# A two-layer decoder on one core: the last unit of the first mixture in two halves of its positions, and the batch attention of the first blocks among the experts of the second half

## The chip, the cores and the metric

One core of a Trainium2 chip runs the whole network as one program, in fp32. The metric is the device time of one execution in microseconds (us). The profile is one execution recorded by the hardware profiler; its times count from the start of its span.

Engines in the text: PE multiplies matrices, DVE and POOL work on vectors, ACT evaluates functions and copies, SP issues most DMAs. Matmul results land in PSUM, which has eight banks of 128 x 512 fp32.

## The reference

The input x has 16 batches of 128 positions of width 128. Every sublayer is added to its input and normalised. The first layer has an attention by a triangular recursion, a cross attention to a context, and a mixture of experts; the second has an attention, a linear mix with the context, and another mixture. Cut to what matters here:

```python
# first layer, mixture: two of 8 experts for each row, and one shared expert
logits = xf @ gate_w.T
topk_logits, topk_idx = jax.lax.top_k(logits, 2)
topk_w = jax.nn.softmax(topk_logits)
comb = zeros(N, 8).at[arange(N)[:, None], topk_idx].add(topk_w)
for e in range(8):
    g = xf @ wg[e].T                 # 128 -> 192
    u = xf @ wu[e].T
    out = out + comb[:, e:e + 1] * (silu(g) * u @ w_down[e].T)
shared = silu(xf @ sg_gate.T) * (xf @ sg_up.T) @ sg_down.T
x = layernorm(x + shared + out)

# second layer, attention: the first axis of x, the batches, is the sequence;
# 16 heads of width 8, separately at each of the 128 positions
qkv = einsum('sbe,fe->sbf', x, in_proj_weight)
probs = softmax(einsum('sbhd,tbhd->bhst', q, k) / sqrt(8))
x = layernorm(x + einsum('bhst,tbhd->sbhd', probs, v) @ out_weight.T)

# second layer, the rest
x = layernorm(x + part1(x) + mean_of_context_part + b)
x = layernorm(x + top1_of_8_experts(x))          # gelu, 128 -> 512 -> 128
```

## The kernel before

The 16 batches are handled in four units of four batches (512 rows; a unit is `g4` in the code, `G = 4`, `NS = 3` is the number of the last). The first two sublayers run unit by unit. A tile scheduler sees all steps in the order in which the functions issue them and reorders within what its own costs and the dependencies allow; each engine then executes its list in order. `weave(one, other)` issues two lists of steps in proportion, one step of the first and then its share of the second.

**The first mixture** works in two ways.

- Units 0 to 2 are routed. Their rows, sorted by expert, fill 31 tiles of 128 rows (`NT0`), handled in eight quads, the last of three tiles. For tile `j`, `fetch(j)` has SP load the weights of its expert in three DMAs (`wu`, and `wd` twice) into one of eight buffers. `gather` lets POOL collect the rows; `up(q)` flips them, multiplies up and calls `gated` (SiLU on ACT, product on DVE); `scatter(q)` multiplies down, copies the result out of PSUM (`y`, L1199) and lets POOL scatter it to memory (`ys`, L1202). `tiles(q)` issues the up of quad q, then the down and scatter of quad q-1, and then the fetches that need the buffers which this down frees.
- Unit 3 is dense. All eight experts run over all its rows, and each result is added to `acc` with its weight from `comb`. `dense(e)` issues the up of expert `e` at full width (three matmuls of 128x512, in PSUM banks `pg_e`, `pu_e`, `pt_e`), then the down of expert `e-1` (eight matmuls of 128x128 into `py_e`, L1109 and L1110), then four additions on DVE. All PSUM tiles of this stage turn through eight shared banks.

`combine(g4)` reads the two results of each row of a routed unit back (`both`, by ACT's queue or SP's, L1211), adds them with eight DVE instructions (L1218), and normalises into `x3`. `by_position(g4)` flips `x3` on PE (L197) and copies it (L198) to `x3p`, laid out as feature, position, batch.

The sequence at the end of the mixture is:

```python
choices()
up_all(f"s{NS}", sup, NS); tiles(3); down_all(NS)
weave([tiles 4 .. 8], [dense 0 .. 3])
weave([dense 4 .. 8], [combine 0, combine 1, by_position 0, combine 2, by_position 1, by_position 2])
layernorm(x3[NS], acc[NS], ..., act=True)
by_position(NS)
```

**The batch attention** needs all 16 batches of a position, so nothing of it starts before the last `by_position`. It has four blocks of 32 positions (`PB`), and seven stages for each, each named by a letter:

- I, `inputs`: q, k, v of the block (L1286 to L1289), and masked copies of q (`qm`) and v (`vm`).
- S, `both_scores`: 256 small score matmuls, `psc` (32x64 with 16 columns, L1317), and the softmax on DVE, ACT and POOL.
- T, `turn_`: the weights flipped on PE (`pbt`, L1345) and copied out.
- M, `mixed`: 256 small matmuls of weights and v (`pbo`, L1361), combined to `ob`.
- P, `project`: the output projection plus the residual (`pob`), and a layernorm.
- L, `linear` (`pc`, L1401), and G, `logits` (`plr`, L1413): the linear sublayer, and the routing logits `lg` of the last mixture.

A PSUM pool `bpsum` opens for it, with 4 banks for `in` (I and M), 2 for `sc` (scores) and 2 for `rest` (T, P, L, G). The order of the stages is written out as words:

```
I0 I1 S0 I2 S1 T0 M0 I3 S2 T1 P0 M1 S3 T2 P1 M2 L0 T3 P2 M3 L1 G0 P3 L2 G1 L3 G2 G3
```

After G3 come the sort by expert and the last mixture.

Of the kernel before, what the change touches and what calls it, by code (L numbers as in the profile page):

```python
# [9 lines left out]
F32 = mybir.dt.float32  # L10
# [12 lines left out]
G = 4  # L23
NG = B // G
E = 8
# [23 lines left out]
def tile_decoder(ctx: ExitStack, tc: tile.TileContext, a, out):  # L49
# [778 lines left out]
    def routed(g4):  # L828

        flip(x2T[g4], x2[g4], f"x2_{g4}", where=where[0])  # L830
        ps = bank([128, G, E], f"plg_{g4}", *where[0])
        for g in range(G):
            PE.matmul(ps[:, g, :], lhsT=x2T[g4][:, g, :], rhs=gw, start=True, stop=True)
        V.tensor_copy(lg0[:, g4 * G : (g4 + 1) * G, :], ps)
# [228 lines left out]
    def by_position(g4):  # L1063
        flip(
            x3p[:, :, g4 * G : (g4 + 1) * G].rearrange("p t g -> p g t"), x3[g4], f"x3_{g4}",
            S.copy if g4 % 2 else V.tensor_copy,
        )


    with tc.tile_pool(name="mix", bufs=2, side="right") as mp:  # L1070
# [14 lines left out]
        h2s = [mp.tile([128, 512], F32, bufs=1, name=f"h2_{k}") for k in range(4)]  # L1085
# [7 lines left out]
        def gated(key, pg, pu, pt, n, kind):  # L1093
            h1 = mp.tile([128, 512], F32, tag=f"h1_{kind}", name=f"h1_{key}")
# [18 lines left out]
        def up_all(key, ws, g4):  # L1113
# [6 lines left out]
            gated(key, pg, pu, pt, 512, 1)  # L1120

        def shared(g4):
            up_all(f"s{g4}", sup, g4)
            if g4:
                down_all(g4 - 1)

# [10 lines left out]
        def dense(e):  # L1137

            if e < E:
                up_all(f"e{e}", dup[:, e], NS)  # L1140
            if not e:
                return
            py = down(f"e{e - 1}", [ddn[:, e - 1]] * G, G)
            for g in range(G):
                V.scalar_tensor_tensor(
                    acc[NS][:, g], py[:, g], comb[:, g, e - 1 : e], acc[NS][:, g], ALU.mult, ALU.add
                )

# [90 lines left out]
        for q in range(4):  # L1239
# [6 lines left out]
        up_all(f"s{NS}", sup, NS)  # L1246
        tiles(3)
        down_all(NS)
        FIRST = 4
        weave(  # L1250
            [(tiles, q) for q in range(4, nq + 1)], [(dense, e) for e in range(FIRST)],
        )
        weave(
            [(dense, e) for e in range(FIRST, E + 1)],
            [(combine, 0), (combine, 1), (by_position, 0), (combine, 2), (by_position, 1),
             (by_position, 2)],
        )
        layernorm(x3[NS], acc[NS], f"x3_{NS}", act=True)
        by_position(NS)
    last.close()  # L1260

    banks.close()
    banks = ExitStack()
    psum[:] = [banks.enter_context(tc.tile_pool(name="bpsum", bufs=2, space=bass.MemoryType.PSUM))]
    last = ExitStack()  # L1270
    lp = last.enter_context(tc.tile_pool(name="last", bufs=2, side="right"))
    with tc.tile_pool(name="batt", bufs=2, side="right") as bp:
# [5 lines left out]
        PB = 32  # L1278
        qms, kps, vms, pss, wgt, turned, ots_, x4s = {}, {}, {}, {}, {}, {}, {}, {}

        def inputs(k):


            xs_ = x3p[:, k * PB : (k + 1) * PB, :].rearrange("p t s -> p (t s)")
            pq, pk, pv = (bank([128, 512], f"p{n}_b{k}", "in", 4) for n in "qkv")
            PE.matmul(pq, lhsT=ipw[:, 0:D], rhs=xs_, start=True, stop=True)  # L1286
            PE.matmul(pk, lhsT=ipw[:, D : 2 * D], rhs=xs_, start=True, stop=True)  # L1287
            for b in range(4):
                PE.matmul(  # L1289
                    pv[:, b * D : (b + 1) * D], lhsT=xs_[:, b * 128 : (b + 1) * 128],  # L1290
                    rhs=ipw[:, 2 * D :], start=True, stop=True,
                )
            qm = qms[k] = bp.tile([128, PB, 4, B], F32, tag="qm", name=f"qm_{k}")
            for q in range(4):
                src = pq.rearrange("p (t s) -> p t s", s=B)
                if q % 2:
                    S.mul(qm[:, :, q, :], src, quarter[:, q : q + 1])
                else:
                    V.tensor_scalar(qm[:, :, q, :], src, quarter[:, q : q + 1], None, ALU.mult)
            kp = kps[k] = bp.tile([128, PB, B], F32, tag="kp", name=f"kp_{k}")  # L1300
            S.copy(kp.rearrange("p t s -> p (t s)"), pk)
# [323 lines left out]
```

## Time and profile before

| | us |
|---|---|
| median of three runs | 976.67 |
| lowest and highest | 974.72, 983.05 |
| time of the profiled run | 976.67 |
| span of the profiled run | 975.0 |
| granted clock of PE over the span | 0.886 of full |
| busy of the span: PE, DVE, POOL, ACT | 809.9, 648.3, 499.8, 477.8 |
| last copy of a routed tile's result out of PSUM starts | 730.82 |
| first combine of a routed unit starts | 741.87 |
| block 0 of the batch attention starts | 768.18 |

The span goes from the first to the last recorded event; the run's own time is 1.67 us longer. "PEclk" or "granted clock" is the share of full speed that the throttle let PE have, and its single values are 1.00 and 0.50. A line of the timeline gives the start, the length, the engine, the line in the code, the operation, its result and operands by name, and in brackets the idle time before it with what ended it. A line of the waits gives what an engine waited for: the sum, how often, and the longest.

### The profile page before, as it was taken

What the parts mean: (1) busy time and instruction counts of PE and PEld (TensorE: products, weight loads), DVE (VectorE), ACT (ScalarE), POOL (GpSimd) and SP (SyncE); (2) the same over time, 40 slices, a digit from 0 to 9 for tenths busy, and PEclk for the clock granted to TensorE, in tenths of its full rate; (3) what the DMA queues carried; (4) which work ended last, traced back from release to release, by engine and by line L of the source; (5) the groups of instructions that cost most, each with busy time, mean ns of one, the idle gap of its engine ahead of it and who ended that gap; (6) DMA issues with size and microseconds to landing.
All of it is one profiled execution on the core that took longest, in us unless ns stands there. A gap on an engine that the chain in (4) does not pass through costs nothing. (4 is left out here: it accounts for less than half of the span.)

```text
span 975.0 us, 33400 instructions
## 1 busy us (share of the span) xinstructions
PE 809.9 (83%) x13626; PEld 602.7 (62%) x13626; DVE 648.3 (66%) x1875; ACT 477.8 (49%) x1617; POOL 499.8 (51%) x669
## 2 busy tenths in 40 slices
PE   4898789999999998999988788588899798771993
PEld 2545257667576676766666567467776487660893
DVE  4258878897797977988665768755357555636452
ACT  5351055354663547544465775545225523540683
POOL 5288766695586946878642413375441010002653
PEclk9689799899998999999997988988999757775897
DMA  4000000000000000000100000175532000006680
GB/s 111 21 0 1 0 2 4 3 3 2 3 4 3 3 2 3 4 3 3 47 23 24 13 14 13 34 221 112 160 101 66 1 4 4 3 1 188 197 251 15
DMA packets 35273, 40.64 MB, mean 42 GB/s; under 512 B 6495, under 2 KB 25454, under 8 KB 35120
## 3 DMA queue, kind: packets, MB, share of 16 engines
q1 hardware_dynamic: 27808, 29.75, 10.0%
q0 software_dynamic: 3456, 6.22, 2.9%
q10 hardware_dynamic: 3856, 2.52, 0.9%
q8 instruction: 108, 1.77, 0.8%
q14 instruction: 45, 0.37, 0.1%
HBM read 33.98 MB, written 5.41 MB: 40 GB/s over the span
## 5 line engine op out<-in xcount | busy, mean ns | idle before, releaser
L561 ACT ACTIVATE ls<-psl,mx 128x8 f32<-128x8 f32 (+15 forms) x512 | 156.8, 317 | 118.1 <-DVE mx L558 104.7
L568 POOL TENSOR_TENSOR ls<-ls,sm 128x32 f32<-128x32 f32 (+15 forms) x128 | 86.2, 673 | 144.8 <-DVE sm L565 125.9
L582 ACT COPY pt<-psp 32x512 f32<-32x512 f32 (+3 forms) x128 | 73.9, 577 | 72.6 <-PE psp L576 72.2
L561 ACT ACTIVATION_READ_ACCUMULATOR ls<-psl,mx 128x1 f32 x512 | 103.9, 203 | 0.0
L509 PEld LDWEIGHTS psl<-kT,qp 32*32 32x32 f32 x3840 | 66.8, 108 | 52.2 <-issue 20.3
L576 PE MATMUL psp<-ident,ls 128*64 128x128 f32 (+3 forms) x512 | 86.0, 292 | 11.8 <-POOL ls L568 9.4
L509 PE MATMUL psl<-kT,qp 32*32 32x8 f32 (+14 forms) x3840 | 88.8, 223 | 4.9 <-DVE psl L538 2.6
L509 PE MATMUL psu<-kT,qp 32*32 32x8 f32 (+13 forms) x3584 | 81.6, 220 | 9.7 <-DVE kT L550 9.1
L463 POOL TENSOR_TENSOR zi<-X,w 128x512 f32<-128x512 f32 x56 | 71.0, 1267 | 29.1 <-PE psq L465 22.8
L509 PEld LDWEIGHTS psu<-kT,qp 32*32 32x32 f32 x3584 | 65.0, 109 | 23.2 <-DVE kT L550 13.0
L465 PE MATMUL psi<-zi,same 128*128 128x512 f32 x128 | 71.7, 643 | 6.6 <-POOL zi L463 3.8
L576 PEld LDWEIGHTS psp<-ident,ls 128*64 128x64 f32 (+3 forms) x512 | 49.1, 122 | 29.8 <-POOL ls L568 12.9
L435 POOL TENSOR_TENSOR pr<-X,raw 128x64 f32<-128x64 f32 (+7 forms) x64 | 55.6, 871 | 19.5 <-DVE X L479 18.8
L463 POOL TENSOR_TENSOR zq<-X,w 128x64 f32<-128x64 f32 (+7 forms) x64 | 55.2, 863 | 7.3 <-PE psk L465 3.6
L525 DVE TENSOR_TENSOR qp<-X,quarter 128x512 f32<-128x512 f32 x48 | 58.7, 1239 | 0.0
L558 DVE TENSOR_REDUCE mx<-psl 128x4 f32<-128x32 f32 (+15 forms) x128 | 55.0, 430 | 3.9 <-PE psl L509 3.4
L1488 POOL DMA_INDIRECT xin<-xs,takes x23 | 21.9, 953 | 67.3 <-DMA w<-in_f_w 58.3
L465 PE MATMUL psq<-zq,same 128*128 128x64 f32 (+7 forms) x128 | 47.3, 453 | 9.5 <-DVE X L479 5.8
L550 DVE COPY kT<-psu 128x32 f32<-128x32 f32 (+13 forms) x112 | 44.5, 398 | 13.9 <-PE psl L509 9.4
L463 POOL TENSOR_TENSOR zk<-K,w 128x64 f32<-128x64 f32 (+6 forms) x56 | 49.0, 874 | 9.0 <-PE psi L465 7.9
L471 DVE TENSOR_TENSOR psi<-psi,wb 128x512 f32<-128x512 f32 x64 | 44.3, 692 | 12.8 <-PE psi L465 12.6
L590 PE MATMUL pso<-pt,vals 64*32 64x128 f32 (+3 forms) x1024 | 40.6, 304 | 9.9 <-ACT pt L582 9.9
(455 smaller groups left out, 1989.3 us busy)
## 6 DMA issues: line engine op xcount, KB each, us to landing
w<-in_f_w SPq DMA_DIRECT2D x46, 256.0 KB, 4.3
wu<-in_m_up SPq DMA_DIRECT2D x31, 192.0 KB, 2.6
wd<-in_m_dn SPq DMA_DIRECT2D x31, 64.0 KB, 2.0
dup<-in_m_up SPq DMA_DIRECT2D x4, 384.0 KB, 6.6
xs<-x5w SPq DMA_DIRECT2D x4, 264.0 KB
ctxT<-in_ctxT SPq DMA_DIRECT2D x4, 256.0 KB, 5.0
mi<-in_mask SPq DMA_DIRECT2D x4, 256.0 KB, 3.0
both<-ys ACTq DMA_DIRECT2D x2, 512.0 KB, 5.2
```

The source lines that it names most:

```text
L435: P.tensor_tensor(pairs[r][:, j:C, j % 4, :], X[r][:, j:C, :], bc(raw[:, j, :], 1, C - j), ALU.mult)
L463: P.tensor_tensor(z[:, :n], src, bc(w[:, r, s, :], 1, n), ALU.mult)
L465: PE.matmul(flat2(ps[:, :n]), lhsT=same, rhs=flat2(z[:, :n]), start=True, stop=True)
L471: V.tensor_tensor(ps[:, :n], ps[:, :n], bc(wb[:, r, s, :], 1, n), ALU.mult)
L509: PE.matmul(ps[js, g, : keys[g].shape[-1]], lhsT=ws_[js, g].rearrange("p q k -> p (q k)"), rhs=keys[g][js], start=True, stop=True,)
L525: (P if g4 == NG - 1 else V).tensor_tensor(qp[:, k], bc(src.rearrange("p s n -> p n s"), 2, 4), bc(bc(quarter, 1, 4 * G), 3, C), ALU.mult,)
L550: V.tensor_copy(kr[:, :, :i, :].rearrange("p g c k -> p g (c k)"), pu[:, :, :n])
L558: V.tensor_reduce(mx, pl[:, :, :m], AX.X, ALU.max, negate=True)
L561: S.activation(ls[:, g, :m], pl[:, g, :m], AF.Exp, bias=mx[:, g : g + 1], accum_out=sm[:, g : g + 1],)
L568: P.tensor_tensor(ls[:, :, :m], ls[:, :, :m], bc(sm, 2, m), ALU.mult)
L576: PE.transpose(pp[:, g, :], ls[:, g, :n], ident)
L582: S.copy(pt[:n, :, :, ks], pp.rearrange("p g (h k) -> p g h k", k=C))
```

## The change

The last unit of the mixture is worked in two halves, `h = 0` for positions 0 to 63 and `h = 1` for positions 64 to 127 of its four batches. Its transposed rows `x2T[3]` are laid out half by half. `dense(h, e)` runs the shared expert first and then the eight experts over the 256 rows of one half. The gate and up results of a step share one bank (`pgu`); a second bank, `rest_`, holds the third up matmul's result and the down's result of the step before. The residual enters through a matmul with the identity, and DVE copies the shared result to `acc`.

Half 0 stands where the shared expert and the first dense experts stood: its first four steps among quads 3 to 7 and the last scatter, its other steps among the combines. Then a PSUM pool `mpsum` replaces the eight shared banks: one bank each for the two dense tags, 3 for `in`, 2 for `sc`, 1 for `rest`. Half 0 is normalised and flipped. Now the second half's dense steps are woven with stages of blocks 0 and 1 of the attention, whose positions lie in half 0: I0 S0 I1 T0 S1 M0 P0 T1. After the second half's norm and flip the old pool `bpsum` opens, and the remaining stages follow in a new order.

The functions of the attention stages are moved ahead of the mixture unchanged, apart from the numbers of banks, which come from `beside`, and apart from `x4T`, `x5T` and `yc`, which live in a pool of their own (`tail`). The core of the diff:

```diff
     def routed(g4):
...
+            flip(
+                flat(x2T[g4]).rearrange("p (h g t) -> p g h t", h=2, g=G), x2[g4], f"x2_{g4}",
+                lambda dst, ps: S.copy(dst, ps.rearrange("p g (h t) -> p g h t", h=2)),
+                where=where[0],
+            )
...
+    def half_by_position(h, place):
+
+        ps = bank([128, 2, 128], f"fl_x3_{NS}_{h}", *place)
+        for k in range(2):
+            PE.transpose(ps[:, k, :], x3[NS][:, 2 * h + k, :], ident)
+        V.tensor_copy(
+            x3p[:, h * 64 : (h + 1) * 64, BS:].rearrange("p t g -> p g t"),
+            ps.rearrange("p k (g t) -> p (k g) t", g=2),
+        )
...
+        def up_half(key, ws, h, rest):
+
+            pgu = bank([128, 2, 256], f"pgu_{key}", *dense_banks[0])
+            pt = rest[:, 0]
+            for ps, c in ((pgu[:, 0], 0), (pt, 2), (pgu[:, 1], 1)):
+                PE.matmul(
+                    ps, lhsT=ws[:, c * 128 : (c + 1) * 128],
+                    rhs=flat(x2T[NS])[:, h * 256 : (h + 1) * 256], start=True, stop=True,
+                )
+            gated(key, pgu[:, 0], pgu[:, 1], pt, 256, 1)
...
-        def dense(e):
-
-            if e < E:
-                up_all(f"e{e}", dup[:, e], NS)
+        def dense(h, e):
+
+
+            order = [E] + list(range(E))
+            rest = bank([128, 2, 256], f"rest_{h}_{e}", *dense_banks[1])
+            if e <= E:
+                n = order[e]
+                up_half(f"e{h}_{n}", sup if n == E else dup[:, n], h, rest)
             if not e:
                 return
-            py = down(f"e{e - 1}", [ddn[:, e - 1]] * G, G)
-            for g in range(G):
+            n = order[e - 1]
+            h1, h2 = hid.pop(f"e{h}_{n}")
+            py = rest[:, 1].rearrange("p (k d) -> p k d", k=2)
+            ws = sdn if n == E else ddn[:, n]
+            for k in range(2):
+                ts, i = slice(k * 128, (k + 1) * 128), 2 * h + k
+                if n == E:
+
+                    PE.matmul(py[:, k], lhsT=x2T[NS][:, i], rhs=ident, start=True, stop=False)
+                PE.matmul(py[:, k], lhsT=h1[:, ts], rhs=ws[:, 0], start=n < E, stop=False)
+                PE.matmul(py[:, k], lhsT=h2[:, ts], rhs=ws[:, 1], start=False, stop=True)
+            if n == E:
+                V.tensor_copy(acc[NS][:, 2 * h : 2 * h + 2], py)
+                return
+            for k in range(2):
+                i = 2 * h + k
                 V.scalar_tensor_tensor(
-                    acc[NS][:, g], py[:, g], comb[:, g, e - 1 : e], acc[NS][:, g], ALU.mult, ALU.add
-                )
+                    acc[NS][:, i], py[:, k], comb[:, i, n : n + 1], acc[NS][:, i], ALU.mult, ALU.add
+                )
+
+        def half_norm(h):
+            hs = slice(2 * h, 2 * h + 2)
+            layernorm(x3[NS][:, hs], acc[NS][:, hs], f"x3_{NS}_{h}", 2, act=True)
...
         choices()
-        up_all(f"s{NS}", sup, NS)
-        tiles(3)
-        down_all(NS)
         FIRST = 4
         weave(
-            [(tiles, q) for q in range(4, nq + 1)], [(dense, e) for e in range(FIRST)],
+            [(tiles, q) for q in range(3, nq + 1)], [(dense, 0, e) for e in range(FIRST)],
         )
         weave(
-            [(dense, e) for e in range(FIRST, E + 1)],
-            [(combine, 0), (combine, 1), (by_position, 0), (combine, 2), (by_position, 1),
-             (by_position, 2)],
+            [(dense, 0, e) for e in range(FIRST, E + 2)],
+            [(combine, 0), (combine, 1), (by_position, 0), (combine, 2), (by_position, 1)],
         )
-        layernorm(x3[NS], acc[NS], f"x3_{NS}", act=True)
-        by_position(NS)
+
+        banks.close()
+        banks = ExitStack()
+        psum[:] = [banks.enter_context(tc.tile_pool(name="mpsum", bufs=1, space=bass.MemoryType.PSUM))]
+        dense_banks[:] = ("du", 1), ("dt", 1)
+        beside.update({"in": 3, "sc": 2, "rest": 1})
+        half_norm(0)
+        weave(
+            [(dense, 1, 0), (by_position, 2, ("rest", 1)), (dense, 1, 1),
+             (half_by_position, 0, ("rest", 1))]
+            + [(dense, 1, e) for e in range(2, E + 2)] + [(half_norm, 1)],
+            [(mark, 0)] * 4 + [(stages[w[0]], int(w[1])) for w in "I0 S0 I1 T0 S1 M0 P0 T1".split()],
+        )
+        half_by_position(1, ("rest", 1))
     last.close()
...
+    beside.update({"in": 4, "sc": 2, "rest": 2})
...
-            "I0 I1 S0 I2 S1 T0 M0 I3 S2 T1 P0 M1 S3 T2 P1 M2 L0 T3 P2 M3 L1 G0 P3 L2 G1 L3 G2 G3"
...
+        for word in "M1 L0 P1 I2 I3 S2 L1 T2 G0 S3 M2 G1 T3 P2 M3 L2 P3 G2 L3 G3".split():
```

`mark` does nothing: the four marks keep the first four steps of the second list empty.

## The prediction

> **What bounds the kernel now.** I read the page first (PE busy 83% of the span, the critical chain spread over many lines, no engine full), then cut the stretch that the change touches into stages, and asked the busy table for each. Columns: stretch, length, busy us of PE, of its weight loads, of DVE, ACT, POOL, granted clock, DMA share, GB/s.
>
> ```profile
> core 0: us, PE busy (x) PEld busy (x) DVE busy (x) ACT busy (x) POOL busy (x), PEclk, DMA share, GB/s
> 681.00:731.00 50.00, 44.28 (x302) 35.93 (x301) 20.69 (x36) 13.29 (x23) 23.62 (x24) 1.00 0.45 131
> 731.00:742.00 11.00, 11.00 (x51) 6.88 (x50) 4.40 (x10) 3.56 (x6) 2.95 (x3) 1.00 0.32 99
> 742.00:768.00 26.00, 18.58 (x93) 11.89 (x91) 22.59 (x96) 18.25 (x31) 0.25 (x4) 0.89 0.06 20
> 768.00:815.00 47.00, 44.27 (x1137) 35.27 (x1138) 24.37 (x47) 17.56 (x30) 4.14 (x4) 0.70 0.01 3
> 815.00:851.00 36.00, 27.28 (x1074) 24.90 (x1055) 21.12 (x86) 17.36 (x40) 4.15 (x4) 0.76 0.02 4
> 851.00:879.00 28.00, 19.74 (x97) 16.95 (x96) 10.96 (x56) 12.86 (x29) 0.00 (x0) 0.68 0.00 1
> ```
>
> Four limits follow each other. To 742 it is PE: routed tiles, then dense experts. From 742 to 768 it is DVE (22.6 of 26), which combines three groups and adds the last experts. From 768 PE again, in the batch attention, at a clock of 0.70; then chains of small steps. The timeline gives the joints:
>
> ```profile
> 730.82 0.56 DVE L1199 COPY y<-py 128x384 f32<-128x384 f32 x1 [0.21 <-PE py L1110]
> 734.24 0.98 POOL L1202 DMA_INDIRECT ys<-y,goes_a  x1 [0.30 <-issue]
> 736.62 0.39 SPq L1211 DMA_DIRECT2D both<-ys  x1
> 741.87 1.14 DVE L1218 SCALAR_TENSOR_TENSOR acc<-both,p,acc 128x128 f32<-128x128 f32 x4 [2.00 <-DMA both<-ys]
> 763.91 3.17 PE L197 MATMUL fl_x<-ident,xa 128*128 128x128 f32 x8 [4.60 <-ACT xa L182]
> 768.18 2.08 PE L1286 MATMUL pq_b<-x3p,sb_ip_w 128*128 128x512 f32 x2 [1.10 <-ACT x3p L198]
> ```
>
> Read it as one chain: the last tile's result leaves PSUM at 730.8, is scattered, read back, and DVE can combine from 741.9 (11.05 us of latency). Only then comes the final layernorm; its flip waited 4.6 us, and attention starts at 768.18. Logits end at 878.26, and 96.7 us follow that nothing in the change touches. The profiled run took 976.67 us over a span of 975.0, and equals the median of the three, so the sum is made against 976.7. A measurement of this kernel tells about 1% (9.8 us) from no change.
>
> **Part 1, before the last tile's result.** The last unit's shared expert and experts were issued among the tiles at full width; now three half-width dense steps and the shared half stand there. A two-pass matmul at full clock takes 0.86 us at 128x512 and 0.22 at 128x128 (rows of the dense stage), so half an up is 3 x 0.43 = 1.29, half an expert's down 4 x 0.22 = 0.89, and half the shared down 1.34 with the two identity matmuls that now add the residual. Out go the shared expert 4.36, three ups 7.7, two downs 3.6: 15.65. In come three half ups 3.87, 1.34 and 0.89: 6.1. Net 9.6 on a busy PE (44.3 of 50). SP's queue bounds this: tiles fetch in steps of 1.91 us, its stalls at 685.5 to 688.3 and 712.6 to 714.2 were waits for the tiles' downs, and without them the last fetch, now at 717.8, could be near 712, landing 2.6 later; the tile's own work then ends about 719 to 721. I take 721.2 (-9.6); bounds are -4 (SP's stalls stay) and -11. The 11.05 us of scatter and read keep: combine can start at 732.3.
>
> **Part 2, to the start of attention (26.3 us before).** DVE has three groups of combine at 3.45 (10.35), flip copies 2.6, additions of experts 5 to 7 2.6, six products 2.5, half a norm 1.0: 19.1. To that 1.8 of hops through ACT and PE: 21. The other half's additions now come later, and group 2's flip with them. Attention starts at 753.3, 14.9 earlier. A copy of the shared result (DVE, 256 wide) replaces the add with the residual and is inside these numbers.
>
> **Part 3, attention's first blocks among the second half.** Before, block 0's start to block 1's M stage took 46.5 us (768.18 to 814.68). Now the same blocks, without the inputs and scores of blocks 2 and 3, share PE with nine half experts. PE's list: ups 10.3, downs 1.34 + 8 x 0.89 = 8.5, I0 and I1 2 x 2.6, S0 and S1 10, T 2.2, M0 4.1, P0 1.8, flip 0.3: 42.4 at full clock. Added waits come from the smaller pool: 2 + 6 banks instead of 8 (du 1, dt 1, in 3, sc 2, rest 1). I find the flips and turns in a row on the one "rest" bank (P0's bank to the layernorm's end 3.3, then 1.0, 1.0), the third "in" bank missing for M0's second pair 0.9, T0 behind the exponent and POOL's division 1.1, P0 behind its blocks 1.35, S1 behind its masks 1.2: 9.9. PE issues in order: behind each of these waits stand the next half expert's matmuls, and behind those ACT's SiLU and DVE's products. The moved stages issue no DMA, and POOL's divisions meet an idle POOL (4.1 of 47). Hops at the end 1.5. Sum without throttle 53.8.
>
> The clock decides the rest. Two rows show it:
>
> ```profile
> 760.00:765.00 5.00, 1.09 (x3) 0.55 (x3) 3.54 (x24) 3.77 (x9) 0.00 (x0) 0.72 0.00 0
> 780.00:785.00 5.00, 5.00 (x78) 3.41 (x75) 3.06 (x5) 0.00 (x0) 0.00 (x0) 0.50 0.01 3
> ```
>
> The first is idle PE, and the clock falls. The second is PE busy all 5 us, with the small score matmuls (32x64 tiles) just done, and the clock is at half: the scores don't hold it. Of 42.4 us, 28.3 are full-array work that doubles at half clock. Bounds: c = 0.93 (only the 10 us at half clock that follow 763 in the trace) adds 2.1; c = 0.5 adds 28.3, of which the 9.9 of waits are absorbed. The nearest row is 768 to 815, 0.70, with the same scores; a stage that has 18.8 us of dense matmuls between them should hold a little more, and I take 0.75: 28.3/0.75 - 28.3 = 9.4, a third of the waits absorbed (-3). Stage: 53.8 + 6.4 = 60.2, so M1 starts at 813.5 (814.68 before).
>
> **Two rules weighed.** Activation tables. On ACT the table row is
>
> ```profile
> 747.14 1.28 ACT L1097 ACT_TABLE_LOAD   x1
> 748.43 0.60 ACT L1097 ACTIVATE h_e<-pg_e 128x512 f32<-128x512 f32 x1
> ```
>
> so a switch costs 1.29 here until the next activation starts. The Trainium skill, "ScalarE: Activation LUTs" (What ACT_TABLE_LOAD costs), has 1283 ns and a drain of about 1380, 2.66 us in all[...]. This speaks against the change, which puts exponents between the SiLUs of the experts: in the order of issue, from combine to the last softmax's end, I count 15 loads where there were 10. Five more are 6.4 us of ACT by the row, 13.3 by the rule; on the path I count two (before S1's masks and before an exponent), which by the rule would add some 3 us. No drain shows; I use the row.
>
> Clock. "TensorE: Matmul & The Clock Gate" (A second HAM failure mode: psum-queue depth-cycling) says that cycling through few PSUM banks leaves short idle gaps between groups of matmuls, and the clock swings. That is du and dt with one bank each, against eight shared ones. The row against it: from 745 to 750 PE was busy 4.11 of 5 with waits in between, and 1.00 was granted. By that row c would be 0.93 and the total 978.7; by the rule's worst reading 0.5 and 995. My 0.75 stands between, on the scores' row.
>
> **Part 4, M1 to the last logits (63.6 us before).** Added, since it was done earlier before: I2 and I3 5.2, S2 5.5. L and G of the early blocks now fill gaps, PE 4.1 of work. The tail, after the last P, shrinks from 27.9 to 23.3, since two blocks' L and G are out of it. Filled waits give 2 to 3. Sum: 63.6 + 5.2 + 5.5 + 4.1 - 4.6 - 2.5 = 71.3. Instruction fetch is a known gap here and stays, as the bursts are the same:
>
> ```profile
> PE pbo L1361 <- issue: 7.4, 4, 2.1
> PE psc L1317 <- issue: 1.7, 2, 1.0
> ```
>
> Other edits cost nothing I can see: the layout copy of x2T on ACT (four groups, same elements), under the routing; the longer-lived attention tiles only take space.
>
> **Sum.** Part 1 -9.6, part 2 26.3 to 21 (-5.3), part 3 46.5 to 60.2 (+13.7), part 4 63.6 to 71.3 (+7.7): +6.5. The logits end at 884.8, and the time is 976.7 + 6.5, **983 us**. The 15 us won at the start of attention are paid back, since PE's work is the same and now shares a slow clock.
>
> **Rivals.**
> - **Overlap wins, 965.5 (15%).** Waits of part 3 are filled by the other stream and the clock holds at 0.93: 978.7 - 11.4 (waits and hops) - 1.8 (one fetch gap) = 965.5. For it: DVE and ACT have room from 768 (24.4 and 17.6 of 47). Against: one "rest" bank orders everything.
> - **Clock at half all through part 3, 995 (20%).** 28.3 more, less 9.9 absorbed: 72.2 instead of 60.2. Place: the dense matmuls between scores, L1317's kind. For it: the 780 row; against: the 745 row. It makes the change slower by 1% once the clock falls below about 0.70.
> - **SP's queue does not move up, 988.6 (15%).** Part 1 wins 4, not 9.6, as the downs still free the weight buffers late. For it: 2.0 us of waits for weights already. Against: its two stalls were on PE.
> - That the halves don't overlap is excluded: in the order of issue, second-half experts stand between score matmuls.
>
> **Numbers.** The forecast holds 50%, its own range 974 to 992 (c from 0.65 to 0.93 and the waits by half): 35 points within 1%, 13 slower, 2 faster. Rival one: 12 faster, 3 within. Two: 20 slower. Three: 5 within, 10 slower. So faster 0.14, within 0.43, slower 0.43. The range, 966 to 999, reaches to the first and the second rival.
>
> **What would show it.** In the profile after: the three-tile y copy near 721; first pq near 753 (a value of 760 would fail parts 1 or 2); M1's first matmul near 813; clock of 753 to 813 near 0.75 (0.9 and over says rival one, under 0.65 rival two); the last logits near 885; five more table loads of 1.28. Wrong altogether if PE's busy time in 753 to 813 is under 45 us, because waits then rule and not the clock.

## The result, and the profile after

The changed kernel took 1013.5 us (median of four runs, 1005.5 to 1020.3), the kernel before 979.9 beside it: 1.040 times as long, with a 95% interval of 1.034 to 1.046. The forecast was 983 us, and its range ended at 999. The ratios here and below, with their intervals, compare the faster executions of either kernel alone and are not the quotients of the medians beside them, and as the profiled runs of e5, e9, e12 and e14 took 1% to 2.6% more than the median of their kernel, nothing rests on their stage lengths alone.

The profiled run of the changed kernel took 1020.3 us over a span of 1018.6, 43.6 more than the one before. Not all of this belongs to the change. On every engine the two programs issue the same instructions in the same order up to the gathering of the routed rows, apart from a few; the first gather starts at 629.6 us before and at 640.3 after, so 10.7 us were lost in work that is the same (in e1, e2 and e4, whose edits lie behind it, this gather starts at 626.7 to 629.2). From there to the end it is 345.4 and 378.3 us, 32.9 more, which agrees with the 33.7 between the medians. All stages below are counted from that gather or between two events behind it.

The busy table by stage, cut at the changed kernel's own joints (stretch, length, busy us of PE, its weight loads, DVE, ACT and POOL, granted clock, DMA share, GB/s):

```profile
732.60:746.00 13.40, 10.26 (x54) 8.54 (x52) 4.28 (x11) 3.04 (x8) 5.05 (x6) 0.92 0.28 90
746.00:773.70 27.70, 14.63 (x61) 11.64 (x59) 19.05 (x80) 18.01 (x31) 0.00 (x0) 0.73 0.06 20
773.70:841.00 67.30, 56.86 (x956) 46.03 (x958) 33.03 (x92) 23.66 (x46) 4.39 (x8) 0.76 0.01 2
841.00:922.40 81.40, 66.46 (x1464) 56.78 (x1464) 36.90 (x138) 35.22 (x74) 4.19 (x4) 0.63 0.01 3
```

The kernel before, cut at the same events:

```profile
730.80:741.90 11.10, 11.10 (x50) 6.82 (x50) 4.47 (x10) 3.56 (x6) 3.09 (x4) 1.00 0.32 98
741.90:768.20 26.30, 18.70 (x94) 11.99 (x92) 22.69 (x96) 18.38 (x31) 0.25 (x4) 0.89 0.06 20
768.20:814.70 46.50, 43.95 (x1107) 34.95 (x1107) 24.07 (x47) 17.43 (x29) 4.14 (x4) 0.70 0.01 3
814.70:878.30 63.60, 47.33 (x1185) 42.15 (x1184) 31.75 (x138) 30.21 (x68) 4.15 (x4) 0.73 0.01 3
```

And the joints of the changed kernel on the timeline:

```profile
732.56 0.56 DVE L1404 COPY y<-py 128x384 f32<-128x384 f32 x1
738.19 0.98 POOL L1407 DMA_INDIRECT ys<-y,goes_a  x1 [0.30 <-issue]
740.58 0.39 SPq L1416 DMA_DIRECT2D both<-ys  x1
746.00 0.35 DVE L1423 SCALAR_TENSOR_TENSOR acc<-both,p,acc 128x128 f32<-128x128 f32 x1 [3.27 <-DMA both<-ys]
773.67 1.33 PE L1104 MATMUL pq_b<-x3p,sb_ip_w 128*128 128x512 f32 x2 [0.68 <-DVE x3p L1082]
```

| step | before | forecast | after |
|---|---|---|---|
| first gather to the last tile's copy | 101.3 | -9.6 | 92.3 (-9.0) |
| to the first combine | 11.1 | 0 | 13.4 (+2.4) |
| to the start of the attention | 26.3 | -5.3 | 27.7 (+1.4) |
| block 0 to block 1's M | 46.5 | +13.7 | 67.3 (+20.8) |
| to the last logits | 63.6 | +7.7 | 81.4 (+17.8) |
| to the end | 96.7 | 0 | 96.2 (-0.5) |
| sum | 345.4 | +6.5 | 378.3 (+32.9) |

A second account of the same stretch, from the last tile's copy to the last logits, asks what PE did. Take PE's busy time in each stretch times its granted clock as the work at full speed, the rest of the busy time as what the half clock cost, and the remainder as waiting. Before: 93.4 us of work, 27.7 of half clock, 26.4 of waiting, 147.5 in all. After: 105.2, 43.0 and 41.6, 189.8. So 12 us of work have moved behind the last tile, which came 9 us earlier for it, and the rest of the loss is in equal parts waiting (15) and half clock (15). (The clock is a mean over the stretch and not over PE's busy time. Taken instruction by instruction against the record of the clock, the differences are 11 of work, 16 of half clock and 15 of waiting.)

Of the experiments, the first four ran on a chip on which the kernel before took 982 us, the others on chips on which it took 1023 to 1028. There the stages that wait for DMAs were longer (from the last logits to the end 116 to 120 us instead of 96), while the stages compared here are PE's, DVE's and ACT's. Totals are therefore given as ratios to the kernel before on the same chip.

### The profile page after: what moved, and what is told of

It reads as the page before. It is cut to its first block, busy times and chain, and to the rows that moved or that the text cites. A ratio compares the mean times of both kernels' runs of the same rounds, so it can differ in the third digit from the quotient of the medians.

```text
span 1018.6 us, 33590 instructions
## 1 busy us (share of the span) xinstructions
PE 836.9 (82%) x13688; PEld 629.4 (62%) x13688; DVE 652.4 (64%) x1898; ACT 486.0 (48%) x1640; POOL 499.6 (49%) x669
## 4 chain that ended last, share of the span: by engine, by line
PE 49%; DVE 19%; POOL 11%; issue 10%; ACT 9%; DMA 2%; ACTq 0%; POOLq 0%; DVEq 0%
PE psp L576 4%; PE psl L509 4%; PE psi L465 3%; PE psu L509 3%; POOL xin L1377 3%; DVE qp L525 3%; PE psd L443 2%; PE pso L590 2%; ACT ls L561 2%; PE psc L1135 2%; PE psy L606 2%; PE psq L465 2%; DVE X L479 2%; PE pbo L1179 2%; POOL ys L1407 2%
## 5 line engine op out<-in xcount | busy, mean ns | idle before, releaser
L568 POOL TENSOR_TENSOR ls<-ls,sm 128x32 f32<-128x32 f32 (+15 forms) x128 | 86.2, 673 | 148.7 <-DVE sm L565 125.9
L509 PE MATMUL psu<-kT,qp 32*32 32x8 f32 (+13 forms) x3584 | 81.4, 219 | 8.3 <-DVE kT L550 8.3
L1155 POOL TENSOR_TENSOR bsc<-bsc,smb 128x512 f32<-128x512 f32 x8 | 8.3, 1057 | 123.9 <-DVE smb L1154 111.4
L435 POOL TENSOR_TENSOR pr<-X,raw 128x64 f32<-128x64 f32 (+7 forms) x64 | 55.8, 874 | 19.7 <-DVE X L479 19.7
L463 POOL TENSOR_TENSOR zk<-K,w 128x64 f32<-128x64 f32 (+6 forms) x56 | 49.1, 877 | 12.5 <-PE psi L465 10.7
```

The costliest lines, as they stand in the source:

```text
L435: P.tensor_tensor(pairs[r][:, j:C, j % 4, :], X[r][:, j:C, :], bc(raw[:, j, :], 1, C - j), ALU.mult)
L463: P.tensor_tensor(z[:, :n], src, bc(w[:, r, s, :], 1, n), ALU.mult)
L509: PE.matmul(ps[js, g, : keys[g].shape[-1]], lhsT=ws_[js, g].rearrange("p q k -> p (q k)"), rhs=keys[g][js], start=True, stop=True,)
L568: P.tensor_tensor(ls[:, :, :m], ls[:, :, :m], bc(sm, 2, m), ALU.mult)
```

## The experiments

**Halves without weaving (e1).** After half 0 comes half 1, in the eight shared banks, then the attention with the banks and the order of words of the kernel before. In short:

```diff
-        banks.close()
-        banks = ExitStack()
-        psum[:] = [... "mpsum" ...]
...
+        half_norm(0); by_position(2); half_by_position(0, ())
+        for e in range(E + 2):
+            dense(1, e)
+        half_norm(1); half_by_position(1, ())
...
-        for word in "M1 L0 P1 I2 I3 S2 ...
+        for word in "I0 I1 S0 I2 S1 T0 M0 I3 ...
```

> The two halves stay, but the attention is not woven among the experts: half 1 follows half 0 in the same eight PSUM banks, then the attention runs with the banks and the word order of before. Theory (the loss sits where attention and experts share a slow clock, and in the order of the later stages): most of the loss goes; 980 to 990 us, attention from block 0 to the last logits takes about 110 us as before. Rival (the thin halves cost it themselves, through their chains ACT-DVE-PE with PE idle and its clock down): 1000 us or more, with attention starting 155 us or later after the first gather of the routed tiles (138.6 before, 133.4 in the changed kernel).

Measured: 1010.2 us, 1.027 (1.020 to 1.034). Attention starts 164.1 us after the first gather. The busy table of this kernel, from the last tile's copy:

```profile
720.20:733.80 13.60, 9.48 (x54) 7.81 (x52) 4.28 (x11) 3.03 (x8) 5.04 (x6) 1.00 0.29 88
733.80:790.80 57.00, 36.60 (x185) 30.82 (x185) 32.80 (x125) 26.52 (x51) 0.25 (x4) 0.81 0.03 10
790.80:908.30 117.50, 96.93 (x2288) 81.16 (x2288) 55.75 (x183) 47.52 (x97) 8.28 (x8) 0.66 0.01 3
```

My theory fell, and the rival stands. From the last tile's copy to the last logits it is 188.1 us, against 189.8 with the weaving and 147.5 before. Weaving the attention among the experts wins nothing over doing one after the other; the loss is there without it. From the first combine to the attention it is 57.0 us instead of 26.3, with 13 us more of PE's work, 13 more of waiting (20.4 in all) and 5 more of half clock; the attention behind it took 117.5 us at a clock of 0.66 instead of 110.1 at 0.72.

**The order of the remaining stages (e2).** One line: the words after the woven stage are `I2 I3 S2 M1 S3 T2 P1 M2 L0 ...`, as before.

> The changed kernel, with the remaining stages in the order that they have before (I2 I3 S2 M1 S3 T2 P1 M2 L0 ...) instead of the new order. Theory (M1 to the last logits lost 18 us; of these 10 are work that moved in, and 8 a lower clock and an order in which blocks 2 and 3 come late): 4 to 8 us less than the changed kernel, 1005 to 1009. Rival (the order does not matter, PE's work at its clock does): within 2 us of 1013.

Measured: 1013.7 us, 1.029 (1.021 to 1.037). From block 0 to the last logits 146.9 us instead of 148.7, at the same clock of 0.69. The time is the changed kernel's (1013.5); the ratio is 1% lower, and the intervals overlap. The rival holds as far as this can tell: the order is not what costs.

**Fewer experts ahead in the kernel before (e3).** `FIRST = 4` becomes `FIRST = 2`.

> The kernel before with one number changed: two dense steps instead of four stand among the last routed tiles (FIRST = 2). Theory (the part of the change that did what was expected is to take PE work out of the time before the last tile's result): that result leaves PSUM 5 to 8 us earlier, the experts fill the read-back wait, and the whole gets 3 to 6 us faster, 972 or so. Rival (the wait is only handed on to DVE, which then has the same additions to do behind the combines): within 2 us of before.

Measured: 985.2 against 982.1 us, 1.002 (0.998 to 1.005). The tile's copy came 7.8 us earlier (93.5 instead of 101.3 after the gather), and all of it was handed back:

```profile
726.30:741.50 15.20, 14.53 (x69) 9.15 (x68) 4.41 (x9) 3.56 (x6) 6.46 (x7) 1.00 0.26 79
741.50:774.40 32.90, 23.71 (x118) 14.95 (x116) 27.98 (x108) 20.75 (x35) 0.25 (x4) 0.97 0.05 17
774.40:888.90 114.50, 95.00 (x2288) 80.22 (x2288) 56.17 (x184) 47.49 (x97) 8.28 (x8) 0.69 0.01 3
```

Of it, 4.1 us went in the read-back (15.2 instead of 11.1), as the last scatter now started 7.4 us behind the copy instead of 3.4, and 6.6 in the stage behind, where DVE has 28.0 us to do instead of 22.7. That is the first lesson: an earlier last tile is worth nothing where the work taken away from it lands in front of the same attention.

**Keeping PE busy in half 0 (e4).** Three matmul pairs that do nothing, ahead of each down of half 0's last steps:

```diff
+            if not h and e > FIRST:
+                for _ in range(3):
+                    PE.matmul(rest[:, 1], lhsT=dup[:, 0, 0:128],
+                              rhs=flat(x2T[NS])[:, 0:256], start=True, stop=True)
```

> The changed kernel with three more matmul pairs of 128x256 ahead of each down of half 0's last steps (six steps, 1.3 us each at full clock, results overwritten): they fill PE's waits there and do nothing else. Theory (from the first combine to the start of attention a chain of hops decides, with PE waiting 10.5 us; its clock of 0.73 costs little): the stage keeps its 27.7 us within 2, its clock goes to 0.9 or more, and the total is within 3 us of 1013, less if the clock stays high afterwards. Rival (the clock at half is what stretches this stage): 4 to 6 us less. Against both, if PE's work is the limit: 8 us more.

Measured: 1008.2 us, 1.025 (1.018 to 1.032). The stage before the attention and the two parts behind it:

```profile
736.90:767.50 30.60, 19.55 (x89) 15.32 (x88) 19.48 (x82) 20.73 (x34) 0.00 (x0) 0.89 0.06 18
767.50:825.20 57.70, 47.54 (x947) 38.84 (x947) 31.82 (x90) 23.25 (x45) 4.39 (x8) 0.87 0.01 2
825.20:903.20 78.00, 65.67 (x1464) 55.69 (x1464) 36.81 (x138) 34.95 (x74) 4.19 (x4) 0.63 0.01 3
```

About 6.7 us of useless work went in (17.4 us of PE work in that stage instead of 10.7); the stage got 2.9 us longer, its clock rose from 0.73 to 0.89, and from the attention's start to the last logits it was 135.7 us at 0.73 instead of 148.7 at 0.69. But the edit didn't do what was meant. The added matmuls write the bank that the down waits for, and some stand behind the same wait:

```profile
741.57 2.90 PE L1336 MATMUL rest<-x2T,dup 128*128 128x256 f32 x6 [4.56 <-DVE h L1270]
```

PE still waited 11.1 us in the stage, where it was 13.1. Against the second run of the changed kernel (e9, 145.7 us at 0.72) the gain is smaller, and the interval overlaps that of e9. So the clock of that stage rose with the added work, and a clock raised by filling the waits was not tested. The woven stage behind ran at 0.87, but so it did in e7, which adds nothing, and how much of the total the higher clock gives is not settled.

**Each down in its own step's bank (e5, e6, e7).** In the changed kernel the down of expert e-1 is written to the bank that holds the third up result of expert e. The down then stands until ACT and DVE have read the next expert's result from that bank: in e1 one starts at 779.72, as the next expert's product ends at 779.66, while its own was done at 776.87 and PE had been idle for 1.49 us:

```profile
776.45 0.42 DVE L1270 TENSOR_TENSOR h<-h,rest 64x256 f32<-64x256 f32 x1
779.24 0.42 DVE L1270 TENSOR_TENSOR h<-h,rest 64x256 f32<-64x256 f32 x1
779.72 0.49 PE L1339 MATMUL rest<-ddn,h_e 128*128 128x128 f32 x2 [1.49 <-DVE h L1270]
```

The edit puts it in the bank of its own step, in short:

```diff
-            rest = bank([128, 2, 256], f"rest_{h}_{e}", *dense_banks[1])
+            if e <= E:
+                rest = rests[h, e] = bank([128, 2, 256], f"rest_{h}_{e}", *dense_banks[1])
...
-            py = rest[:, 1].rearrange("p (k d) -> p k d", k=2)
+            py = rests[h, e - 1][:, 1].rearrange("p (k d) -> p k d", k=2)
```

e5 is e1 with this edit. e6 is the changed kernel with it in both halves, with `dt` 2 and `in` 2. e7 has it in half 0 alone.

> The halves without woven attention, as in the first experiment, with one difference: an expert's down goes to the free half of the PSUM bank of its own step (which holds its own third up result) instead of the bank of the next step. There it had to wait until ACT and DVE had read the next expert's third up result from the same bank. Theory (this wait is what stretches the halves: PE waited 16.9 us for DVE's products between the last tile's result and the attention): from the first combine to the attention 57.0 us become 43 to 48, total 997 to 1001. Rival (the waits are the chain's own, silu, product and down one after the other): within 3 us of 1010.

> The changed kernel with each down in the bank of its own step, in both halves; half 1 needs two such banks for that, and the attention's inputs get two banks instead of three. Theory (shared bank): the stage before the attention shortens from 27.7 to 23 us or less, the woven stage keeps its length, since PE is busy there; total 1007. Rival (banks for the attention decide the woven stage): with two input banks, the values wait for the masks, and the woven stage gets 3 us or more longer; total 1013 or more.

> The changed kernel with each down in the bank of its own step in half 0 alone; half 1 and the banks of the woven stage as in the changed kernel. Theory: the stage before the attention shortens from 27.7 to 23 us or less, all else stays; total 1008. Rival: within 2 us of 1013.

Measured: e5 1.022 (1.014 to 1.031), e6 1.032 (1.025 to 1.039), e7 1.017 (1.004 to 1.030). In e5 the stage from the first combine to the attention is 49.5 us instead of 57.0 (43 to 48 expected), and PE's waiting in it 12.9 instead of 20.4, which speaks for the wait; but the totals of e1 and e5 don't stand apart. In e6 and e7 that stage is 25.8 and 30.0 us (27.7 and 30.0 in the two runs of the changed kernel), not the 23 expected: with the attention behind it, other waits take its place. With e6's two input banks the woven stage got no longer either (62.7 us to block 1's M, 67.3 and 64.3 in the changed kernel). The shared bank is a part of the loss at most, and not its cause.

**More of half 0 ahead (e8, e13), and more ahead in the kernel before (e14).** `FIRST = 8` in the changed kernel, which undoes the part that took PE work away from the tiles; e13 is that and e7's edit together; e14 is the kernel before with `FIRST = 6`.

> The changed kernel with eight instead of four of half 0's steps among the last routed tiles (FIRST = 8), which undoes the part of the change that took PE work away from there. Theory (PE work is only moved, and half 0's steps cost less where tiles cover their waits): the last tile's result comes 7 to 9 us later, the stage before the attention is 4 to 6 us shorter, total 1010 to 1016. Rival (the early tile result is worth its time): 1020.

> The changed kernel with both repairs: eight of half 0's steps among the tiles (FIRST = 8), and in half 0 each down in its own step's bank. The woven stage is as in the changed kernel. Theory (the causes add: half 0's part is then repaired, and what is left is half 1's 18.8 us of work at a clock near 0.7 with its waits, against what the attention's earlier start saves): 1.010 to 1.020 times the kernel before. Rival (with the steps among the tiles, the shared bank costs nothing any more): as with FIRST = 8 alone, 1.024. Other rival (the woven stage alone holds the loss): 1.03 or more.

> The kernel before with six instead of four dense steps among the last routed tiles (FIRST = 6). Theory (PE work is only moved, at full clock on either side; two steps instead of four gave 1.002): within 0.5% of before. Rival (the wait for the read-back then stands uncovered, and PE's clock falls): 1% or more slower. Other rival (DVE has less to do behind the combines): 3 us faster or more.

Measured: e8 1.024 (1.016 to 1.033), e13 1.022 (1.013 to 1.032), e14 0.996 (0.991 to 1.002). For the changed kernel the undone part is worth about 1.5% by the middle of the ratios (1.024 against 1.040 and 1.038), with an interval that overlaps that of e9 and almost touches the first. The last tile's result came 116.8 us after the gather, 4.6 later than in e6 and e7 on the same chip; 7 to 9 were expected. The busy table of e8:

```profile
748.40:761.50 13.10, 8.00 (x51) 6.64 (x49) 4.32 (x12) 2.27 (x6) 4.91 (x5) 1.00 0.30 92
761.50:780.70 19.20, 7.22 (x21) 4.30 (x21) 14.64 (x68) 10.81 (x23) 0.00 (x0) 0.64 0.09 29
780.70:922.40 141.70, 116.41 (x2414) 96.45 (x2414) 69.36 (x229) 58.84 (x120) 8.57 (x12) 0.72 0.01 2
```

Now the stage ahead of the attention is short (19.2 us), but PE stands idle in 12 us of it, and the long stage behind it is hardly shorter (141.7 us; 148.7 and 145.7 in the changed kernel). e13 adds nothing to e8: with half 0's steps among the tiles, the shared bank is not seen to cost anything. What is left, about 2%, is in the woven stage and behind it.

**What the woven stage costs per expert (e10), beside the changed kernel again (e9).** Experts 4 to 7 are left out of half 1:

```diff
-            if e <= E:
+            if e <= (4 if h else E):
...
-            + [(dense, 1, e) for e in range(2, E + 2)] + [(half_norm, 1)],
+            + [(dense, 1, e) for e in range(2, 6)] + [(half_norm, 1)],
```

> The changed kernel itself, once more, beside the three others on one chip. Expected from its first measurement: 3.4% to 4.6% over the kernel before. From the accounts of the stages: about 85 us of PE work (busy time times granted clock) from the attention's start to the last logits, at a clock near 0.70, and 25 us of idle PE.

> The changed kernel with experts 4 to 7 left out in half 1 (their matmuls, activations and additions; half 1's results lack them). This takes 4 x (1.29 + 0.89) = 8.7 us of PE work at full clock out of the woven stage. Theory (PE is the limit there, at a clock near 0.7; nothing of the experts is hidden in the attention's waits): 8.7/0.7 = 12 us less, 11 to 14. Rival (the attention's chain of waits sets the woven stage and the experts fill its gaps): 5 us less or under.

Measured: e9 1061.2 us, 1.038 (1.026 to 1.051), so the first ratio stands on another chip. Its two parts from the attention's start to the last logits, for comparison with 67.3 and 81.4 us in the first profile:

```profile
808.40:872.70 64.30, 52.96 (x951) 42.34 (x951) 32.78 (x92) 23.67 (x46) 4.39 (x8) 0.83 0.01 2
872.70:954.10 81.40, 66.37 (x1464) 56.69 (x1464) 36.87 (x137) 35.23 (x74) 4.19 (x4) 0.63 0.01 3
```

e10 took 1046.7 us, 14.5 us less, 1.022 (1.007 to 1.038). In it, from the attention's start to the last logits:

```profile
791.20:926.40 135.20, 109.71 (x2358) 91.76 (x2358) 64.13 (x213) 55.78 (x112) 8.57 (x12) 0.67 0.01 2
```

That is 10.5 us less than in e9 and 13.5 less than in the first profile, for 8.7 us of matmuls at full clock. Nothing of the experts is hidden in the attention. PE's waiting, 25.5 us, is the same as with all eight (26.4 and 25.4): the experts do not fill the attention's waits. The theory expected 11 to 14 us less and the rival 5; the two totals, 14.5 us apart, have intervals that overlap, but the stage speaks for the theory.

**Two rest banks (e11).** `in` 2 and `rest` 2 instead of 3 and 1.

> The changed kernel with two PSUM banks for flips, turns and projections in the woven stage and two for the attention's inputs, instead of one and three. Theory of the prediction (the single rest bank orders projection, turns and flip one after the other, PE waited 5.4 us there): idle PE from the attention's start to the last logits falls from 25 to 20 us, total 3 to 5 us less. Rival (the third input bank is worth as much, or PE's clock eats it): within 2 us of the changed kernel.

Measured: 1047.1 us, 1.032 (1.024 to 1.041). PE waited 26.4 us from the attention's start to the last logits, no less. On the waits the rival holds: the one behind the projection goes, and in its place the flip of half 0 waits 3.2 us for its layernorm and the projection 2.1 for its blocks. The price that the prediction put on the rest bank was there, but it covered other waits. The totals don't decide: the medians of e11 and e9 are 14 us apart, more than either forecast had, and the intervals overlap widely.

**A busy PE ahead of the last flip, in the kernel before (e12).**

```diff
+        warm = bank([128, 512], "warm")
+        for _ in range(4):
+            PE.matmul(warm, lhsT=ident, rhs=flat(acc[NS]), start=True, stop=True)
         layernorm(x3[NS], acc[NS], f"x3_{NS}", act=True)
```

> The kernel before with four added matmul pairs of 128x512 (0.86 us each at full clock, results never read) after the last expert's addition, where PE waits 4.6 us for the last layernorm. Theory (the half clock from 762 to 772 comes from this wait): the attention's first inputs run at full clock, 2 us less or up to 5, and 768 to 773 shows a clock near 1. Rival (the clock falls for another reason, or falls later instead): within 1 us of before, or 2 us more where the added matmuls delay the flip.

Measured: 1025.1 against 1025.0 us, 1.001 (0.996 to 1.006). The edit doesn't fill the wait. PE stands as long as before in front of a flip, and the added matmuls come behind it, among the flips:

```profile
810.47 0.86 PE L197 MATMUL fl_x<-ident,xa 128*128 128x128 f32 x2 [4.60 <-ACT xa L182]
811.12 1.92 PE L1260 MATMUL warm<-acc,ident 128*128 128x512 f32 x2
```

So the stage from the first combine to the attention is 30.5 us here instead of 26.3. From block 0 to the last logits, cut behind the first inputs and scores and at block 1's M, this kernel shows

```profile
818.90:828.90 10.00, 9.49 (x280) 7.36 (x280) 4.23 (x6) 4.92 (x8) 0.00 (x0) 1.00 0.01 3
828.90:863.40 34.50, 32.16 (x827) 26.41 (x824) 21.10 (x44) 12.08 (x21) 4.14 (x4) 0.66 0.02 4
863.40:930.80 67.40, 52.45 (x1185) 46.67 (x1184) 30.66 (x134) 30.05 (x68) 4.15 (x4) 0.63 0.01 2
```

and the kernel before, whose third part is the 63.6 us at 0.73 above,

```profile
768.20:782.00 13.80, 12.82 (x280) 9.55 (x280) 4.47 (x7) 5.17 (x8) 0.00 (x0) 0.75 0.01 2
782.00:814.70 32.70, 31.14 (x828) 25.40 (x827) 19.60 (x41) 12.26 (x21) 4.14 (x4) 0.68 0.01 4
```

The first inputs and scores (280 matmuls) ran at full clock and took 10.0 us instead of 13.8, as the theory said. Behind them the clock is lower than before, and at the last logits nothing of the gain is left: 111.9 us instead of 110.1. That speaks for the second rival, that the half clock falls later instead. But the stages of one profile don't carry this alone, and the total can't tell a gain that was lost behind from one that paid for the added matmuls.

No version of the change was as fast as the kernel before, and no variant of the kernel before was measurably faster.

## Why the prediction was wrong

- **Part 1 was right in itself.** The last tile's copy came 9.0 us earlier (forecast 9.6). What failed is **"the 11.05 us of scatter and read keep"**. With the last two copies 3.1 us apart instead of 5.7, POOL scatters the last two quads without a pause, one scatter each 1.29 us; the last starts at 738.19, 5.6 us after the copy, where it was 3.4 (730.82 to 734.24). The first and the last but one of the seven:

```profile
730.46 0.98 POOL L1407 DMA_INDIRECT ys<-y,goes_a  x1 [2.46 <-DVE y L1404]
736.90 0.98 POOL L1407 DMA_INDIRECT ys<-y,goes_a  x1 [0.31 <-issue]
```

  The latency is 13.4 us.
- **Part 2 had the right DVE sum and the wrong limit.** DVE was busy 19.05 us, forecast 19.1. But the stage took 27.7 us and not 21, as the step **"to that 1.8 of hops"** was short by almost 7. Half experts are short jobs in a long chain: up, SiLU on ACT, product on DVE, down. Four rows show what the chain stood behind (ACT twice, then DVE, then PE):

```profile
741.45 0.38 ACT L1268 ACTIVATE h<-rest 64x256 f32<-64x256 f32 x1 [5.02 <-issue]
744.01 0.38 ACT L1267 ACTIVATE h_e<-pgu_e 128x256 f32<-128x256 f32 x1
749.62 0.39 DVE L1269 TENSOR_TENSOR h_e<-h_e,pgu_e 128x256 f32<-128x256 f32 x1
750.70 0.77 PE L1339 MATMUL rest<-ddn,h_e 128*128 128x128 f32 x2 [4.16 <-DVE h L1270]
```

  ACT's SiLU stands behind the DMA that ACT issues at 740.63 for the read-back, once the scatters are done; DVE's product, ready to run from 744.4 on, stands behind the combines, whose first waited for that DMA until 746.00. In the kernel before the same orders exist, but PE had full-width experts to do meanwhile: it was busy all of the 11.1 us of the read-back and 18.7 of the 26.3 behind. Half 0 has too few steps left for that; PE was busy 10.3 of 13.4 and 14.6 of 27.7. The view of PE's waits sums those for these products from 733 to 774:

```profile
PE rest L1339 <- DVE h L1270: 10.5, 3, 4.2
```

  The prediction named what was added there, not what had been filler.
- **Part 3 met the clock and had wrong what it stretches.** Forecast 0.75, measured 0.76, which is in part luck: e9, the same kernel, shows 0.83 in the same stages. The step that failed is **"of 42.4 us, 28.3 are full-array work that doubles at half clock"**: the small matmuls double too. One block of 256 score matmuls took 9.17 us at a granted clock of 0.50, where 250 took 4.25 at 0.90:

```profile
856.43 4.25 PE L1135 MATMUL psc<-kp,qm 32*64 32x16 f32 x250
865.33 9.17 PE L1135 MATMUL psc<-kp,qm 32*64 32x16 f32 x256
```

  The profile before had it already: there the 256 scores from 786.81 on took 5.5 us at a mean clock of 0.74. With all of it at 0.76, 42.4 becomes 55.8; PE's busy time was 56.9. The second error is that **"a third of the waits absorbed (-3)"**: PE waited 10.4 us, close to the 11.4 of waits and hops before that deduction.
- **Part 4 is the largest miss, 10.1 us, and it lies in the clock.** The step that failed is the sum **"63.6 + 5.2 + 5.5 + 4.1 - 4.6 - 2.5"**: it leaves the old stages at their old clock of 0.73 and adds the moved ones at full clock. By the two tables PE had 7 us more work there (busy time times clock, 41.9 instead of 34.6), waited 1 us less, and lost 12 us more to the half clock: 4 on the added work, and 8 on the work that was there before, as the clock fell to 0.63. This is no chance of one run: in e6, e7 and e9 the same stage takes 81.4 to 82.6 us at 0.62 or 0.63. (The 4.1 for L and G is no added work; these stages stood in this part before, and the 4.6 takes them off again. The gaps put down to instruction fetch came to 6.2 us, where they had been 9.1; each of them, before and after, ended 2.2 to 2.7 us after a packet of the instruction queue had started, which fits that reading.)
- **The rivals.** The one with the clock at half through part 3 (995) fell, with 0.76. That SP's queue wouldn't move up fell on the first chip, where the copy came 9.0 us earlier. Overlap did not win: in e10 the four experts in the woven stage cost 10.5 to 13.5 us for 8.7 at full clock.
- **The rule on tables** carries little: the five added loads came as forecast (15 instead of 10 up to the last logits), they took 1.28 us each with no drain behind them, and none of the four rows above waits for one. **The rule on PSUM cycling** spoke against the change and so did the result. But the page that it names has a kernel that cycles through banks in each iteration, and nothing on how few they are, and with other banks in e11 and e6 the clock from the attention's start to the last logits was 0.74 and 0.69 (0.69 and 0.72 in the changed kernel). So the banks are not shown to be what keeps the clock low. In the kernel before, without those pools, the attention ran at 0.70 to 0.73 as well.

Why the attention holds PE at a clock near 0.7 was not tested by an experiment, but the traces show what goes with it. In the 16 profiles the clock changes only in steps of 3.41 us. I cut the time from 30 us ahead of the attention to the last logits into such stretches, 759 in all, and counted in each how long PE was busy with matmuls of 128x128 weights, and how long with any. At half clock, with 2.8 us or more of the full-size ones, the clock rose behind 93 of 98 stretches. Where PE was busy for over 3.2 us but had less than 2.4 of the full-size ones, the rest being scores and M's products, it rose behind 1 of 74. At full clock, with 2.4 us or more of them, it fell behind none of 106; with less than 0.4 it fell behind 49 of 50, among them all 8 in which PE was busy for over 3.2 us. In the changed kernel:

```profile
846.15:849.56 3.41, 3.41 (x33) 2.18 (x20) 1.64 (x6) 1.21 (x3) 0.00 (x0) 0.50 0.02 5
849.56:856.39 6.83, 6.83 (x45) 5.32 (x44) 5.67 (x23) 3.63 (x8) 0.00 (x0) 1.00 0.01 2
856.39:859.80 3.41, 3.41 (x233) 3.37 (x232) 1.75 (x4) 3.41 (x10) 0.00 (x0) 1.00 0.02 5
859.80:893.93 34.13, 30.42 (x628) 27.17 (x621) 15.31 (x43) 14.38 (x24) 4.19 (x4) 0.50 0.01 3
```

PE is busy all of the first three. The first has nearly only full-size matmuls, and the clock rises; the third has only scores, and the clock falls for 34 us. So the prediction's "the scores don't hold it" was right, and it goes for the stages behind the woven one as well. It fits that the full-size matmuls added in e4 and e12 raised the clock beside them and for the next 10 us, and no further.

In short: the dense experts were the filler of a stage in which DVE is the limit, and the cheapest work that PE had, most of it at full clock. Half of them were moved to where PE has no room for them. Woven into the attention, where PE is busy over four fifths of the time at a clock near 0.7, they fill nothing (e10); in a row ahead of it, in the thin steps of one half, they cost as much in work and waits (e1). Which part of those waits is due to the halves being short and which to the shared bank stays open. In e3, where two full-width experts moved behind the last tile, PE's waits from there to the attention were 9.9 us instead of 7.6, in e1 24.5, which speaks for the short halves; e5, with 4.0 + 12.9, speaks for the bank.

## What to carry to other kernels

Before moving work to "overlap" with a stage, ask which engine is the limit in both places and at which granted clock: two experts moved to either side of the last tile cost nothing measurable here (e3 1.002, e14 0.996), and four half experts beside a stage in which PE is busy cost more than their own time (e10). Check what the moved work had covered where it stood (here a read-back of 11 us and DVE's combines). And when the clock is below one, divide all PE time by it, the small matmuls too.

## What the runs showed of the hardware

- The half clock is as costly for 32x64 matmuls of 16 columns as for full tiles: 36 ns each at 0.50 (9.17 us for 256), 17 at 0.90 (4.25 us for 250).
- A PE busy with such small matmuls alone doesn't keep its clock: behind all 8 stretches of 3.41 us with over 3.2 us busy and under 0.4 of it full-size, the granted clock fell from 1.00 to 0.50, and at 0.50 it rose behind 93 of 98 stretches with 2.8 us or more of full-size matmuls. This is read from the traces; no run exchanged the small matmuls for others.
- Four full-size matmul pairs just ahead of a busy stretch kept the clock at 1.00 for the next 10 us, and at the stretch's end nothing was left of it (e12, one profile: 10.0 + 34.5 + 67.4 us, before 13.8 + 32.7 + 63.6).
- POOL issued these scatters at one each 1.29 us. Seven in a row put the last one 5.6 us behind the copy that it waits for (7.4 in e3), where it had been 3.4.
- On chips where the DMA-bound stages were a fifth to a quarter longer (116 to 120 us instead of 96 behind the last logits), the ratio of the changed kernel was the same, 1.038 and 1.040.
